# A linear-attention recurrence in levels: both head parities on the partitions, k masked in place of r

## The chip, the cores and the metric

The kernel runs on one core of a Trainium2 chip. A core has a matrix engine (TensorE, PE in the profile; its weight loads are listed as PEld), a vector engine (VectorE, DVE), an activation engine (ScalarE, ACT), a general engine (GpSimd, POOL) and a queue engine that issues DMAs (SyncE, SP). Each engine has its own instruction queue and runs it in order; semaphores make one engine wait for another. The metric is the time of one execution in microseconds, as the device measures it. All data are fp32.

## The reference

Two layers run over 32 sequences of 128 positions with 512 features. Layer 0 is a cross-attention with normalised inputs. Layer 1 is a block of the RWKV kind: layer norm and token shift, low-rank mixes, projections to r, k, v, a gate g and a decay w, a recurrence with a 16 x 16 state for each of 32 heads, a group norm, an output projection and a feed-forward part. What matters here is the recurrence:

```python
def step(s, rkvw):
    r_t, k_t, v_t, w_t = rkvw
    a = k_t[..., :, None] * v_t[..., None, :]
    out = jnp.einsum('bhi,bhij->bhj', r_t, u * a + s)
    s = a + w_t[..., :, None] * s
    return (s, out)
```

So the output at position t is r_t against the sum, over earlier positions i, of k_i v_i, decayed by the product of the w between i and t, plus the start state decayed, plus the same position's product weighted by u.

## The kernel before, in words

**Tiling.** The sequences go in 8 groups (`NG`) of `G` = 4. Activations lie transposed: 128 features on the partitions (8 heads of 16), and N = 4 x 128 positions of the four sequences along the free dimension. The 512 features make `NC` = 4 chunks, so the recurrence is called 8 x 4 = 32 times (`recurrence`, called from `layer1`). Positions are treated in halves of `C` = 64.

**Levels instead of steps.** The recurrence is not run step by step. At the level l, each block of 2l positions is cut in two; the products of the r of its right half with the k of its left half make a piece of a 64 x 64 matrix per head (`at`), and after each level r in the right half and k in the left half are multiplied by the decays of their half (`twice`, which also halves the table of decay products, `tot`). Before the change the position itself (`x0`, `d0`), neighbours at distance one (`x1`, `d1`) and the level 2 (`x2`, `d2`) are made by elementwise products on DVE, followed by a matmul with `sum_bc`, which adds the 16 features of a head; the levels 4, 8, 16 and 32 (`LEVELS`) are made by TensorE.

**A level on TensorE.** A matmul contracts over 32 partitions, `q * DM` to `(q + 1) * DM`, which hold two heads, an even and an odd one. To keep them apart r is copied twice by ACT with a mask on the partitions (`par`): the copy `r2` holds, side by side, r of the even head with zeros in the odd one's rows, and the reverse, 32 columns each, since only right halves are wanted. For each of 4 sequences, 2 halves `n` and 4 head pairs `q` one matmul has k as stationary operand (32 partitions x 64 positions) and r2 as moving operand (64 columns); the halves n go to the partitions 0 to 63 and 64 to 127 of four PSUM banks `pa[q]`. DVE then copies the wanted entries to `at` under a mask (`copy_predicated`); at the level 32 ACT copies them.

**After the levels.** v is transposed and copied into `vp` in a spaced form: 32 columns for each head pair and parity, half of them zero, with positions of both halves n on the partitions. The value products are `at` against `vp`, in two bunches of 32 matmuls: each contracts over the 64 positions of one half. The state for the second half (`s1`) needs k of the first half transposed (`kt`, 64 partitions), a product with v (`ps`) and a merge under the parity mask (two DVE operations). State products with r are added in the same banks `po`. The result is `acc`.

**What sets the order.** Every operation is first recorded (`Program.record`), with a cost for its engine (`cost`, or a number of ns given with `K.bunch`, which keeps a series of matmuls together), and `schedule` then lists the operations of all engines in an order of its own: it simulates the engines and the slots of the buffers, and moves work earlier where TensorE would idle. The instructions are emitted in that order by `Program.run`, line 229, so nearly every instruction of the profile has line 229; groups are told apart by the names of what they write and read. Buffers come from rings: 54 tiles of 128x512 (`t`), 8 PSUM banks (`bank`), two `rk` tiles with r and k, two `at` tiles for each q, two `vp` tiles, and 4 weight slots (`wring`).

The bunches around the change are: a level, `K.bunch(843)` at lines 887 to 898; the value products, `K.bunch(720)` twice at 983 to 995; the state products, `K.bunch(1020)` at 971; and the new state's product, `K.bunch(385)` at 952.

Of the kernel before, what the change touches and what calls it, by code (L numbers as in the profile page):

```python
# [13 lines left out]
AF = mybir.ActivationFunctionType  # L14
ALU = mybir.AluOpType
# [3 lines left out]
P = 128  # L19
B = 32  # L20
L = 128
E = 512
S = 16
G = 4
NG = B // G
N = G * L
# [2 lines left out]
NH = E // S  # L29
DM, NMIX, DD = 32, 5, 64  # L30
C = 64
LEVELS = (4, 8, 16, 32)
T_SLOTS, SMALL_SLOTS, W_SLOTS = 54, 40, 4
Q4 = 4
EPS = 1e-5

# [503 lines left out]
def xattn_then_rwkv(ctx: ExitStack, tc: tile.TileContext, a: dict, out: bass.AP):  # L540
# [5 lines left out]
    def slots(tag, count, shape, space=const):  # L546
        return [space.tile(shape, F32, tag=f"{tag}{i}", name=f"{tag}{i}") for i in range(count)]
# [4 lines left out]
    rks = Pool(slots("rk", 2, [P, 2 * N]))  # L552
# [18 lines left out]
    ident = const.tile([P, P], F32, tag="ident", name="ident")  # L571
# [29 lines left out]
    sum_bc, par = fixed("sum_bc", [P, H8, S]), fixed("par", [P, 2])  # L601
# [7 lines left out]
    def v_(name, c):  # L609
        i = VECS.index(name)  # L610
        return vec[:, i, c : c + 1]
# [218 lines left out]

    def recurrence(c, ex, xk, xr, xv, wk, wr, s0m):

        rk = View(Tensor(rks, [P, 2, N]))
        r, k = rk[:, 0], rk[:, 1]
        K.scalar.copy(r, proj(wr, xr, c))
        K.scalar.copy(k, proj(wk, xk, c))
        v = wt()
        K.scalar.copy(v, proj(wv, xv, c))

        vp = View(Tensor(vps, [P, G * Q4 * 2 * DM]))
        at = [View(Tensor(p, [P, G * 2, C])) for p in ats]
        pt = bank()
        for b in range(G):
            K.tensor.transpose(pt[:, b * P : (b + 1) * P], v[:, b * P : (b + 1) * P], ident)
        K.scalar.copy(
            vp.view(0, (2 * DM, G * Q4), (DM + S, 2), (1, S)),
            pt.rearrange("p (x y j) -> p x y j", x=G * Q4, y=2),  # L850
        )


        x0, x1 = wt(), wt()
        K.vector.scalar_tensor_tensor(x0, k, v_("u", c), r, ALU.mult, ALU.mult)
        K.vector.tensor_tensor(x1[:, 0 : N // 2], r[:, 1::2], k[:, 0::2], ALU.mult)
        sums = sum_bc.rearrange("p h s -> p (h s)")
        d0, d1 = bank(), bank()
        K.tensor.matmul(d0, sums, x0, start=True, stop=True)
# [1 line left out]
        acc = wt()  # L861

        def twice(h, tot):


            nb = N // (2 * h)
            s = rk.view(h, (N - h, 2), (2 * h, nb), (1, h))
            K.vector.tensor_tensor(s, s, tot.view(0, (1, 2), (2, nb), (0, h)), ALU.mult)
            got = wt([P, nb]) if nb > 64 else st_(nb)
            K.vector.tensor_tensor(got, tot[:, 0 : 2 * nb : 2], tot[:, 1 : 2 * nb : 2], ALU.mult)  # L870
            return got

        tot = twice(1, ex)

        nb = N // 4
        x2 = wt()
        K.vector.tensor_tensor(
            x2.view(0, (4, nb), (2, 2), (1, 2)),
            rk.view(2, (4, nb), (1, 2), (0, 2)),
            rk.view(N, (4, nb), (0, 2), (1, 2)), ALU.mult,  # L880
        )
        d2 = bank()
        K.tensor.matmul(d2, sums, x2, start=True, stop=True)
        tot = twice(2, tot)

        for li, l in enumerate(LEVELS):

            r2 = wt([P, G * 2, C])
            nb = C // (2 * l)
            for x in range(2):  # L890
                K.scalar.activation(
                    r2.view(x * (C // 2), (C, G * 2), (l, nb), (1, l)),
                    rk.view(l, (C, G * 2), (2 * l, nb), (1, l)),
                    AF.Identity, scale=par[:, x : x + 1],
                )
            pa = [bank() for _ in range(Q4)]
            with K.bunch(843):
                for b in range(G):
                    for n in range(2):
                        for q in range(Q4):  # L900
                            rows_q = slice(q * DM, (q + 1) * DM)
                            K.tensor.matmul(
                                pa[q][n * C : (n + 1) * C, b * C : (b + 1) * C],
                                rk[rows_q, 1, b * L + n * C : b * L + (n + 1) * C],
                                r2[rows_q, 2 * b + n],
                                start=True, stop=True,
                            )
            for q in range(Q4):
                if l < C // 2:
                    K.vector.copy_predicated(  # L910
                        at[q].view(l, (C, 2 * G), (2 * l, nb), (1, l)),
                        level[l].view(0, (0, 2 * G), (l, nb), (1, l)),
                        pa[q].view(0, (C // 2, 2 * G), (l, nb), (1, l)),
                    )
                else:
                    for n in range(2):
                        sl = slice(n * C, n * C + l)
                        K.scalar.copy(
                            at[q][sl, :, l : 2 * l],
                            pa[q][sl, 0 : N // 2].rearrange("p (x t) -> p x t", t=l),  # L920
                        )
            tot = twice(l, tot)
            if li == 0:
                t1, t2 = wt(), wt()
# [5 lines left out]
                nb = N // 4  # L930
                K.vector.tensor_tensor(
                    t2.view(0, (4, nb), (2, 2), (1, 2)),
                    d2.view(0, (4, nb), (2, 2), (1, 2)),
                    v.view(0, (4, nb), (0, 2), (1, 2)), ALU.mult,
                )
# [10 lines left out]
        pk = bank()  # L946
        for b in range(G):
            K.tensor.transpose(pk[0:C, b * P : (b + 1) * P], k[:, b * L : b * L + C], ident)
        kt = wt([C, N])
        K.scalar.copy(kt, pk[0:C, :])  # L950
        ps = bank()
        with K.bunch(385):
            for b in range(G):
                for q in range(Q4):
                    K.tensor.matmul(
                        ps[q * DM : (q + 1) * DM, b * DM : (b + 1) * DM],
                        kt[:, b * P + q * DM : b * P + (q + 1) * DM],
                        vp[0:C].view((b * Q4 + q) * 2 * DM, (DM + S, 2), (1, S)),
                        start=True, stop=True,
                    )  # L960
        s1 = wt([P, G, 2 * S])
        for x in range(2):
            of_x = (x * S, (2 * S, G), (1, S))
            K.vector.scalar_tensor_tensor(
                s1.view(*of_x), ps.view(*of_x), par[:, x : x + 1], s0t.view(*of_x),
                ALU.mult, ALU.add,
            )


        po = [bank() for _ in range(2)]  # L970
        with K.bunch(1020):
            for b in range(G):
                for n in range(2):
                    for q in range(Q4):
# [5 lines left out]
                            r[sl, b * L + n * C : b * L + (n + 1) * C],  # L980
                            start=(b == 0), stop=False, skip_group_check=True,
                        )
        for half in range(2):
            with K.bunch(720):
                for b in range(half * G // 2, (half + 1) * G // 2):
                    for x in range(2):
                        for n in range(2):
                            for q in range(Q4):
                                sl = slice(n * C, (n + 1) * C)
                                i = (b * Q4 + q) * 2 * DM + x * DM  # L990
                                K.tensor.matmul(
                                    po[n][q * DM : (q + 1) * DM, b * C : (b + 1) * C],
                                    vp[sl, i : i + DM], at[q][sl, 2 * b + x, :],
                                    start=False, stop=(x == 1), skip_group_check=True,
                                )
        for n in range(2):
            o = acc.view(n * C, (L, G), (1, C))
            K.vector.tensor_tensor(
# [263 lines left out]
```

## Time and profile before

| what | value |
|---|---|
| median of 3 runs | 1839.58 us (1839.23 to 1839.6) |
| the profiled execution | 1843.41 us |
| its span | 1841.7 us |
| PE busy | 1796.9 us (98%) |
| PE weight loads busy | 888.9 us (48%) |
| DVE busy | 1227.2 us (67%) |
| ACT busy | 751.2 us (41%) |
| POOL busy | 309.8 us (17%) |

The profile comes from one execution. The span runs from the first to the last instruction. Groups of instructions are listed with what they write and read (`bank<-t,rk` writes a PSUM bank and reads a t tile and an rk tile), for matmuls with the rows and columns of the array in use (`32*64`) and the moving operand (`32x64`), the count, the busy time in us, the mean ns of one instruction, and the idle time of the engine ahead of them with what ended it. Every fp32 matmul appears twice, each time with a weight load, and transposes once. The ends of matmuls are modelled, so a matmul's listed length includes the way through the array, and pieces are best measured from start to start. One group of four sequences takes about 228 us; its recurrence stage, from the first level to the last of its four calls, about 100 us (334 to 435 us in the second group).

### The profile page before, as it was taken

To read this page: it belongs to the slowest core of one execution; us is meant where nothing else is said; L and a number is where in the kernel's file an instruction comes from. 1 tells how busy PE (TensorE), PEld (TensorE's weight loads), DVE (VectorE), ACT (ScalarE), POOL (GpSimd) and SP (SyncE) were. 2 spreads that over 40 slices of the span, in tenths; PEclk is the share of its full clock that TensorE was granted. 3 is DMA by queue.
4 is the path that set the end of the run, shared out by engine and by line. 5 is a ranking of instruction groups with operands and counts; after the bars stand their busy time and mean duration, and the time that the engine had idled before them with its cause. 6 is when DMAs were issued, how large, how long until landed. Compare 5 with 4: busy or idle time off the path is not lost.

```text
span 1841.7 us, 46377 instructions
## 1 busy us (share of the span) xinstructions
PE 1796.9 (98%) x20264; PEld 888.9 (48%) x20264; DVE 1227.2 (67%) x2754; ACT 751.2 (41%) x1501; POOL 309.8 (17%) x329
## 2 busy tenths in 40 slices
PE   8999999999999999999999999999999999999998
PEld 4345543555435554355543555435554455445543
DVE  8857883678746786567855678556784567866652
ACT  5345621546225462254522644225452355425421
POOL 2420014000150001500025000240002400240011
PEclk9999999999999999999999999999999999999999
DMA  7001102021110201211011120111201111001000
GB/s 229 1 25 47 52 23 92 25 64 35 46 69 25 73 26 46 69 38 60 25 52 63 40 71 13 52 63 40 71 13 57 58 40 48 2 23 48 26 18 29
DMA packets 61947, 87.29 MB, mean 47 GB/s; under 512 B 20336, under 2 KB 21488, under 8 KB 61744
## 3 DMA queue, kind: packets, MB, share of 16 engines
q1 hardware_dynamic: 61024, 84.06, 14.1%
q8 instruction: 159, 2.61, 0.6%
q14 instruction: 44, 0.36, 0.1%
q10 hardware_dynamic: 720, 0.26, 0.1%
HBM read 75.93 MB, written 8.39 MB: 46 GB/s over the span
## 4 chain that ended last, share of the span: by engine, by line
PE 89%; DVE 6%; ACT 2%; POOL 2%; issue 1%; POOLq 0%; DVEq 0%; ACTq 0%
PE bank L229 89%; DVE t L229 5%; ACT t L229 1%; POOL t L229 1%; DVE small L229 1%; ACT at L229 0%; POOL small L229 0%; DVE at L557 0%; DVE rk L229 0%; DVE at L229 0%; POOLq L1258 0%; ACT L229 0%; DVE vp L557 0%; ACT rk L229 0%; DVE fold L229 0%
## 5 line engine op out<-in xcount | busy, mean ns | idle before, releaser
L229 PE MATMUL bank<-t,wring 128*128 128x512 f32 x1024 | 488.4, 605 | 4.0 <-ACT t L229 2.0
L229 PE MATMUL bank<-wring,t 128*128 128x512 f32 x768 | 341.0, 601 | 8.5 <-DVE t L229 8.5
L229 POOL TENSOR_TENSOR t<-t,t 128x512 f32<-128x512 f32 x192 | 242.8, 1299 | 435.1 <-DVE t L229 422.5
L229 DVE TENSOR_TENSOR t<-bank,t 128x512 f32<-128x512 f32 (+1 forms) x256 | 147.2, 585 | 225.6 <-PE bank L229 194.7
L229 PEld LDWEIGHTS bank<-t,wring 128*128 128x128 f32 x1024 | 182.0, 190 | 221.2 <-issue 167.7
L229 PE MATMUL bank<-t,t 128*128 128x512 f32 x512 | 261.6, 614 | 1.2 <-ACT t L229 1.2
L229 POOL TENSOR_TENSOR small<-small,neg_half 128x1 f32<-128x1 f32 (+1 forms) x96 | 59.3, 632 | 1091.6 <-DVE small L229 1072.7
L229 PEld LDWEIGHTS bank<-wring,t 128*128 128x128 f32 x768 | 146.3, 192 | 197.9 <-issue 179.5
L229 ACT ACTIVATE t<-bank 128x512 f32<-128x512 f32 x120 | 71.8, 598 | 368.2 <-PE bank L229 368.0
L229 ACT COPY t<-bank 128x512 f32<-128x512 f32 (+1 forms) x240 | 135.1, 587 | 201.7 <-PE bank L229 200.3
L229 ACT ACTIVATE t<-rk,par 128x256 f32<-128x256 f32 x256 | 116.7, 501 | 130.0 <-DVE rk L229 116.3
L229 PE MATMUL bank<-ident,t 128*128 128x128 f32 x900 | 140.5, 278 | 6.8 <-DVE t L229 6.7
L229 ACT ACTIVATE t<-bank,small 128x512 f32<-128x512 f32 x128 | 87.9, 689 | 140.4 <-DVE small L229 139.9
L229 PEld LDWEIGHTS bank<-ident,t 128*128 128x128 f32 x900 | 104.3, 140 | 81.1 <-issue 46.4
L229 DVE COPY_PREDICATED at<-level,bank 128x256 f32<-128x256 int32 x384 | 142.7, 426 | 0.0
L229 DVE SCALAR_TENSOR_TENSOR t<-bank,vec,t 128x512 f32<-128x512 f32 x192 | 131.3, 742 | 16.1 <-PE bank L229 16.1
L229 PEld LDWEIGHTS bank<-t,rk 32*64 32x64 f32 x8192 | 99.7, 130 | 82.3 <-ACT t L229 54.3
L229 PE MATMUL bank<-t,wv 128*128 128x512 f32 x256 | 128.6, 601 | 0.0
L229 PEld LDWEIGHTS bank<-t,t 128*128 128x128 f32 x512 | 85.0, 191 | 77.9 <-issue 35.9
L229 PE MATMUL bank<-t,rk 32*64 32x64 f32 x8192 | 117.9, 230 | 2.9 <-issue 2.9
L229 DVE TENSOR_REDUCE small<-bank 128x1 f32<-128x512 f32 x128 | 87.8, 686 | 41.1 <-PE bank L229 40.6
L229 ACT COPY at<-bank 32x256 f32<-32x256 f32 x256 | 87.8, 361 | 24.1 <-PE bank L229 21.3
(94 smaller groups left out, 1882.5 us busy)
## 6 DMA issues: line engine op xcount, KB each, us to landing
t<-in_ctx_dram SPq DMA_DIRECT2D x32, 256.0 KB, 3.1
t<-in_x_dram SPq DMA_DIRECT2D x32, 256.0 KB, 2.8
wring<-in_WrT_dram SPq DMA_DIRECT2D x8, 1024.0 KB, 5.3
wring<-in_WkT_dram SPq DMA_DIRECT2D x8, 1024.0 KB, 5.2
wring<-in_WgT_dram SPq DMA_DIRECT2D x8, 1024.0 KB, 5.0
wring<-in_WoT_dram SPq DMA_DIRECT2D x8, 1024.0 KB, 5.3
out_dram<-t SPq DMA_DIRECT2D x32, 256.0 KB, 2.0
wring<-in_WfkT_dram SPq DMA_DIRECT2D x7, 1024.0 KB, 5.0
```

The source lines that it names most:

```text
L229: f(*[real(x) for x in args], **{k: real(x) for k, x in kw.items()})
```

## The change

The two head parities move from the moving operand to the stationary one, and so to the partitions of the result.

- The `rk` tile grows from 2N to 3N columns: r, then k twice for each half of 64 positions, once with the odd heads' rows zeroed and once with the even heads'. Two masked ACT copies from the projection's PSUM bank write k; the masked copies of r at each level go.
- A level's matmul has 32 partitions x 128 columns of k as stationary operand and the 32 right-half positions of r, read in place, as moving operand. The result has 128 partitions (parity, position) x 32 columns.
- The level 2 becomes a TensorE level as well: `LEVELS` begins with 2, and the products `x2`, `d2`, `t2` go.
- `twice` multiplies k on DVE (two operations for the levels 2 to 16, one for 1 and 32), and r on GpSimd (POOL).
- `vp` is written by four copies of 64 partitions; parity and position are its partitions. The value products become one bunch of 32 matmuls over 128 partitions.
- k of the first half is transposed with both parities, and `s1` is one addition.
- The ring of t tiles has 52 tiles in place of 54.

```diff
-LEVELS = (4, 8, 16, 32)
-T_SLOTS, SMALL_SLOTS, W_SLOTS = 54, 40, 4
+LEVELS = (2, 4, 8, 16, 32)
+T_SLOTS, SMALL_SLOTS, W_SLOTS = 52, 40, 4
...
-        K.scalar.copy(k, proj(wk, xk, c))
+        pk = proj(wk, xk, c)
+        for x in range(2):
+            K.scalar.activation(
+                rk.view(N + x * C, (2 * C, 2 * G), (1, C)),
+                pk.rearrange("p (n s) -> p n s", s=C), AF.Identity, scale=par[:, x : x + 1],
+            )
...
-        K.scalar.copy(
-            vp.view(0, (2 * DM, G * Q4), (DM + S, 2), (1, S)),
-            pt.rearrange("p (x y j) -> p x y j", x=G * Q4, y=2),
-        )
+        for n in range(2):
+            for x in range(2):
+                K.scalar.copy(
+                    vp[x * C : (x + 1) * C].view(
+                        n * Q4 * DM + x * S, (2 * Q4 * DM, G), (DM, Q4), (1, S)
+                    ),
+                    pt[n * C : (n + 1) * C].view(x * S, (P, G), (DM, Q4), (1, S)),
+                )
...
-        K.vector.scalar_tensor_tensor(x0, k, v_("u", c), r, ALU.mult, ALU.mult)
-        K.vector.tensor_tensor(x1[:, 0 : N // 2], r[:, 1::2], k[:, 0::2], ALU.mult)
+        K.vector.scalar_tensor_tensor(x0, pk, v_("u", c), r, ALU.mult, ALU.mult)
+        K.vector.tensor_tensor(x1[:, 0 : N // 2], pk[:, 0::2], r[:, 1::2], ALU.mult)
...
-            nb = N // (2 * h)
-            s = rk.view(h, (N - h, 2), (2 * h, nb), (1, h))
-            K.vector.tensor_tensor(s, s, tot.view(0, (1, 2), (2, nb), (0, h)), ALU.mult)
+            nb, of = N // (2 * h), C // (2 * h)
+            if of == 1 or h == 1:
+                k2 = rk.view(N, (2 * C, 2 * G), (C, 2), (2 * h if h == 1 else 1, of if h == 1 else h))
+                by = tot.view(1, (2 * of, 2 * G), (0, 2), (2 if h == 1 else 0, of if h == 1 else h))
+                K.vector.tensor_tensor(k2, k2, by, ALU.mult)
+            else:
+                for x in range(2):
+                    k2 = rk.view(N + x * C, (2 * C, 2 * G), (2 * h, of), (1, h))
+                    by = tot.view(1, (2 * of, 2 * G), (2, of), (0, h))
+                    K.vector.tensor_tensor(k2, k2, by, ALU.mult)
+            r1 = rk.view(h, (2 * h, nb), (1, h))
+            K.gpsimd.tensor_tensor(r1, r1, tot.view(0, (2, nb), (0, h)), ALU.mult)
...
-        x2 = wt()
-        K.vector.tensor_tensor(
-            x2.view(0, (4, nb), (2, 2), (1, 2)),
-            rk.view(2, (4, nb), (1, 2), (0, 2)),
-            rk.view(N, (4, nb), (0, 2), (1, 2)), ALU.mult,
-        )
-        d2 = bank()
-        K.tensor.matmul(d2, sums, x2, start=True, stop=True)
...
-            r2 = wt([P, G * 2, C])
-            for x in range(2):
-                K.scalar.activation(
-                    r2.view(x * (C // 2), (C, G * 2), (l, nb), (1, l)),
-                    rk.view(l, (C, G * 2), (2 * l, nb), (1, l)),
-                    AF.Identity, scale=par[:, x : x + 1],
-                )
...
                             K.tensor.matmul(
-                                pa[q][n * C : (n + 1) * C, b * C : (b + 1) * C],
-                                rk[rows_q, 1, b * L + n * C : b * L + (n + 1) * C],
-                                r2[rows_q, 2 * b + n],
+                                pa[q][:, i : i + C // 2],
+                                rows[:, N + 2 * at_ : N + 2 * at_ + 2 * C],
+                                rows.view(at_ + l, (2 * l, nb), (1, l)),
                                 start=True, stop=True,
                             )
...
-                t2.view(0, (4, nb), (2, 2), (1, 2)),
-                d2.view(0, (4, nb), (2, 2), (1, 2)),
-                v.view(0, (4, nb), (0, 2), (1, 2)), ALU.mult,
-            right = acc.view(2, (4, nb), (1, 2))
-            for s in range(2):
-                K.vector.tensor_tensor(right, right, t2.view(s, (4, nb), (2, 2)), ALU.add)
...
-        for x in range(2):
-            of_x = (x * S, (2 * S, G), (1, S))
-            K.vector.scalar_tensor_tensor(
-                s1.view(*of_x), ps.view(*of_x), par[:, x : x + 1], s0t.view(*of_x),
-                ALU.mult, ALU.add,
-            )
+        K.vector.tensor_tensor(
+            s1, ps[:, 0 : G * DM].rearrange("p (b x) -> p b x", b=G), s0t, ALU.add
+        )
...
-        for half in range(2):
-            with K.bunch(720):
-                for b in range(half * G // 2, (half + 1) * G // 2):
-                    for x in range(2):
-                        for n in range(2):
-                            for q in range(Q4):
-                                sl = slice(n * C, (n + 1) * C)
-                                i = (b * Q4 + q) * 2 * DM + x * DM
-                                K.tensor.matmul(
-                                    po[n][q * DM : (q + 1) * DM, b * C : (b + 1) * C],
-                                    vp[sl, i : i + DM], at[q][sl, 2 * b + x, :],
-                                    start=False, stop=(x == 1), skip_group_check=True,
-                                )
+        with K.bunch(1000):
+            for b in range(G):
+                for n in range(2):
+                    for q in range(Q4):
+                        i = ((2 * b + n) * Q4 + q) * DM
+                        K.tensor.matmul(
+                            po[n][q * DM : (q + 1) * DM, b * C : (b + 1) * C],
+                            vp[:, i : i + DM], at[q][:, 2 * b + n, :],
+                            start=False, stop=True, skip_group_check=True,
+                        )
```

More of the change, by code (lines that the diff above doesn't have):

```diff
@@ L551, in xattn_then_rwkv @@
     small = Pool(slots("small", SMALL_SLOTS, [P, 64]))
-    rks = Pool(slots("rk", 2, [P, 2 * N]))
+    rks = Pool(slots("rk", 2, [P, 3 * N]))
     weights = Pool(slots("wring", W_SLOTS, [P, NC * E]))
@@ L831, in recurrence @@
     def recurrence(c, ex, xk, xr, xv, wk, wr, s0m):
-        rk = View(Tensor(rks, [P, 2, N]))
-        r, k = rk[:, 0], rk[:, 1]
+        rk = View(Tensor(rks, [P, 3 * N]))
+        r = rk[:, 0:N]
         K.scalar.copy(r, proj(wr, xr, c))
-        K.scalar.copy(k, proj(wk, xk, c))
+        pk = proj(wk, xk, c)
[4 more added lines that the diff above has]
+            )
         v = wt()
         K.scalar.copy(v, proj(wv, xv, c))
-        vp = View(Tensor(vps, [P, G * Q4 * 2 * DM]))
+        vp = View(Tensor(vps, [P, G * 2 * Q4 * DM]))
         at = [View(Tensor(p, [P, G * 2, C])) for p in ats]
@@ L873, in recurrence @@
         tot = twice(1, ex)
-        nb = N // 4
-        x2 = wt()
-        K.vector.tensor_tensor(
-            x2.view(0, (4, nb), (2, 2), (1, 2)),
-            rk.view(2, (4, nb), (1, 2), (0, 2)),
-            rk.view(N, (4, nb), (0, 2), (1, 2)), ALU.mult,
-        )
-        d2 = bank()
-        K.tensor.matmul(d2, sums, x2, start=True, stop=True)
-        tot = twice(2, tot)
         for li, l in enumerate(LEVELS):
-            r2 = wt([P, G * 2, C])
+            pa = [bank() for _ in range(Q4)]
             nb = C // (2 * l)
-            for x in range(2):
-                K.scalar.activation(
-                    r2.view(x * (C // 2), (C, G * 2), (l, nb), (1, l)),
-                    rk.view(l, (C, G * 2), (2 * l, nb), (1, l)),
-                    AF.Identity, scale=par[:, x : x + 1],
-                )
-            pa = [bank() for _ in range(Q4)]
             with K.bunch(843):
@@ L900, in recurrence @@
                         for q in range(Q4):
-                            rows_q = slice(q * DM, (q + 1) * DM)
+                            rows = rk[q * DM : (q + 1) * DM]
+                            at_ = b * L + n * C
+                            i = (2 * b + n) * (C // 2)
                             K.tensor.matmul(
-                                pa[q][n * C : (n + 1) * C, b * C : (b + 1) * C],
-                                rk[rows_q, 1, b * L + n * C : b * L + (n + 1) * C],
-                                r2[rows_q, 2 * b + n],
+                                pa[q][:, i : i + C // 2],
+                                rows[:, N + 2 * at_ : N + 2 * at_ + 2 * C],
+                                rows.view(at_ + l, (2 * l, nb), (1, l)),
                                 start=True, stop=True,
@@ L915, in recurrence @@
                 else:
-                    for n in range(2):
-                        sl = slice(n * C, n * C + l)
+                    for x in range(2):
+                        sl = slice(x * C, x * C + l)
                         K.scalar.copy(
@@ L923, in recurrence @@
             if li == 0:
-                t1, t2 = wt(), wt()
+                t1 = wt()
                 K.vector.tensor_tensor(acc, d0, v, ALU.mult)
@@ L929, in recurrence @@
                 K.vector.tensor_tensor(acc[:, 1::2], acc[:, 1::2], t1[:, 0 : N // 2], ALU.add)
-                nb = N // 4
-                K.vector.tensor_tensor(
-                    t2.view(0, (4, nb), (2, 2), (1, 2)),
-                    d2.view(0, (4, nb), (2, 2), (1, 2)),
-                    v.view(0, (4, nb), (0, 2), (1, 2)), ALU.mult,
-                )
-                right = acc.view(2, (4, nb), (1, 2))
-                for s in range(2):
-                    K.vector.tensor_tensor(right, right, t2.view(s, (4, nb), (2, 2)), ALU.add)
         s0t = wt([P, G, 2 * S])
@@ L945, in recurrence @@
         )
-        pk = bank()
+        pt = bank()
         for b in range(G):
-            K.tensor.transpose(pk[0:C, b * P : (b + 1) * P], k[:, b * L : b * L + C], ident)
-        kt = wt([C, N])
-        K.scalar.copy(kt, pk[0:C, :])
+            K.tensor.transpose(
+                pt[:, b * P : (b + 1) * P], rk[:, N + 2 * b * L : N + 2 * b * L + 2 * C], ident
+            )
+        kt = wt()
+        K.scalar.copy(kt, pt)
         ps = bank()
@@ L954, in recurrence @@
                 for q in range(Q4):
+                    i = (2 * b * Q4 + q) * DM
                     K.tensor.matmul(
                         ps[q * DM : (q + 1) * DM, b * DM : (b + 1) * DM],
-                        kt[:, b * P + q * DM : b * P + (q + 1) * DM],
-                        vp[0:C].view((b * Q4 + q) * 2 * DM, (DM + S, 2), (1, S)),
+                        kt[:, b * P + q * DM : b * P + (q + 1) * DM], vp[:, i : i + DM],
                         start=True, stop=True,
@@ L982, in recurrence @@
                         )
-        for half in range(2):
-            with K.bunch(720):
-                for b in range(half * G // 2, (half + 1) * G // 2):
-                    for x in range(2):
-                        for n in range(2):
-                            for q in range(Q4):
-                                sl = slice(n * C, (n + 1) * C)
-                                i = (b * Q4 + q) * 2 * DM + x * DM
-                                K.tensor.matmul(
-                                    po[n][q * DM : (q + 1) * DM, b * C : (b + 1) * C],
-                                    vp[sl, i : i + DM], at[q][sl, 2 * b + x, :],
-                                    start=False, stop=(x == 1), skip_group_check=True,
-                                )
+        with K.bunch(1000):
[7 more added lines that the diff above has]
+                            start=False, stop=True, skip_group_check=True,
+                        )
         for n in range(2):
```

## The prediction

> **What bounds the kernel now.** I read the page's first part and its chain of waits, then the groups with shapes kept apart, then the timeline of one recurrence. First the page: TensorE (PE) is busy for 98% of the span, and the chain that ended last is 89% PE.
>
> ```profile
> span 1841.7 us, 46377 instructions
> PE 1796.9 (98%) x20264; PEld 888.9 (48%) x20264; DVE 1227.2 (67%) x2754; ACT 751.2 (41%) x1501; POOL 309.8 (17%) x329
> PE 89%; DVE 6%; ACT 2%; POOL 2%; issue 1%; POOLq 0%; DVEq 0%; ACTq 0%
> ```
>
> So PE time added or removed moves the end one for one, and the other engines have room: DVE a third, ACT more than half, POOL four fifths. The chain in order of time says the same of the stage that is changed: one unbroken stretch of PE work covers the first levels.
>
> ```profile
> 306.89 73.81 PE bank L229 x814
> ```
>
> Next, what PE spends on the pieces that the change touches. These are timeline lines (start, length, ..., tile rows*columns, moving operand, count). A length includes the tail of the last matmul, so a piece costs the distance to the next start.
>
> ```profile
> 334.48 0.91 PE L229 MATMUL bank<-t,rk 32*64 32x64 f32 x64
> 335.32 1.12 PE L229 MATMUL bank<-t,wv 128*128 128x512 f32 x2
> ...
> 350.27 0.46 PE L229 MATMUL bank<-vp,t 64*32 64x32 f32 x32
> 350.65 1.12 PE L229 MATMUL bank<-t,t 128*128 128x512 f32 x2
> 351.71 1.09 PE L229 MATMUL bank<-rk,t 32*32 32x64 f32 x64
> 352.74 1.13 PE L229 MATMUL bank<-t,wring 128*128 128x512 f32 x2
> 353.79 0.86 PE L229 MATMUL bank<-at,vp 64*32 64x64 f32 x64
> 354.58 1.12 PE L229 MATMUL bank<-t,t 128*128 128x512 f32 x2
> ```
>
> A level (32 matmuls, 64 in the trace because each fp32 matmul appears twice, with two weight loads) takes 335.32 - 334.48 = 0.84 us; half of the value products 0.79; the state products 352.74 - 351.71 = 1.03; the new state's product 0.38. Last, the weight loads (PEld) by width, and the loads of the one group that already uses 32-row, 128-column tiles:
>
> ```profile
> L229 PEld LDWEIGHTS bank<-t,rk 32*64 32x64 f32 x8192 | 99.7, 130 | 82.3 <-ACT t L229 54.3 <-issue 22.5 <-ACT at L229 2.0
> L229 PEld LDWEIGHTS bank<-rk,t 32*32 32x32 f32 x2048 | 30.0, 105 | 19.9 <-issue 11.5 <-DVE t L229 6.0 <-DVE at L229 1.5
> L229 PEld LDWEIGHTS bank<-t,w2a 32*128 32x128 f32 x256 | 10.1, 183 | 21.7 <-DVE t L229 7.6 <-issue 7.1 <-DVE small L229 5.3
> 308.80 0.31 PEld L229 LDWEIGHTS bank<-t,w2a 32*128 32x128 f32 x8 [0.76 <-DVE t L229]
> 910.63 1.05 PE L229 MATMUL bank<-wol,t 128*128 128x128 f32 x8
> ```
>
> A load of 32 columns lasts 105 ns, of 64 130, of 128 183: about 0.81 ns a column. Eight loads of 128 columns, two on each of four row tiles, take 0.31 us. The four tiles load side by side (one after another would take far longer), but the second load of a tile begins only when the first has passed: 0.31 - 0.18 leaves 0.13, less some 0.02 for the fourth tile's later start, so about **0.11 us per load and tile**. That fits 128 x 0.81 = 0.104.
>
> **The change part by part (PE).**
>
> *Level products.* A level stays 32 matmuls, but each loads 32x128 weights and streams 32 columns, where it loaded 32x64 and streamed 64. The eight tiles of 32*64 become four of 32*128, so a tile takes 16 loads in place of 8. Streaming is cheap: 512-column matmuls on full tiles go at 0.43 us each in the trace (the 32 from 914.96 on take 14.00 us), so 0.84 ns a column, and 32 columns are 0.027 us against a load of 0.108. I price the level by its loads: 16 x 0.108 = 1.73, plus what a bunch has around its steady part. The state bunch gives that: 16 rounds of 64 columns on four tiles are 16 x 0.0535 = 0.86 of its 1.03, so 0.17. Together 1.90 us. From below, with start and tail hidden, 1.73. From above, load and matmul one after the other in a tile: 16 x (0.108 + 0.027) + 0.17 = 2.33. I take 1.90, because the load is covered by the matmul elsewhere in the trace: the eight 128-column instructions above on one full tile take 1.05 us, (1.05 - 0.29) / 7 = 0.109 each (0.29 is the mean of one), with a load of 0.108 and a stream of 0.107 each. There are five levels in place of four, and 8 x 4 = 32 recurrences: 5 x 1.90 x 32 = 304.0 against 4 x 0.84 x 32 = 107.5: **+196.5 us**.
>
> The Trainium skill ("TensorE: Matmul & The Clock Gate", The mechanism, in the part on row and column tiling) says that a weight load overlaps running matmuls only where their row group differs. In a level the load that follows on a tile always has the row group of that tile's matmul, so by this rule load and matmul would add and the total would be about 2060, the upper price. The 0.109 us row, load and matmul on the same rows, disagrees, and I go by the row.
>
> *The pair level's product.* The d2 matmul (128x512, two instructions of 0.43) goes: 0.86 x 32 = **-27.3 us**.
>
> *Value products.* Two bunches of 0.79 become one of 32 matmuls, each 128*32 with 64 columns on four column tiles. The state bunch has this count, width of load and stream: 1.03. Bounds: 0.86 (streams alone) and 1.2 (the state bunch with another 0.17). -(1.58 - 1.03) x 32 = **-17.6 us**.
>
> *Others.* The new state's product keeps 16 matmuls on four column tiles; the k transpose doubles its width of load but not its stream (four cost 0.63 with 64-column weights, 0.66 with 128): 0. Bunches per recurrence stay eight (5 + 1 + 1 + 1 against 4 + 1 + 1 + 2), so the changes of tile shape around them cost the same.
>
> Sum on PE: 196.5 - 27.3 - 17.6 = **+151.6 us**.
>
> **The other engines**, which cost nothing while PE covers them:
>
> - ACT: 256 masked copies of r go (116.7 us busy); k takes two masked 128x512 activations for one copy (+0.7 us), vp four 64x256 copies of about 0.36 for one of 0.59 (+0.9): -116.7 + 51 = -65 us.
> - DVE: four more predicated copies per recurrence (142.7 us over 384, so 0.37 each: +1.5 us); the pair level's product, its value product and two adds go (0.68 + 0.68 + 2 x 0.42 = 2.2); the doublings of k alone take two operations of 0.69 and eight of 0.42, 4.7 against 6 x 0.69 = 4.1; s1 is one operation for two (-0.25). About -0.35 us each: -11 us.
> - POOL: 192 doublings of r, 128x256, at half of the 1.30 us row: +125 us, to about 435 of 1990.
>
> *A wait that is added.* Each doubling of r now runs on POOL while DVE doubles k, and the next level waits for both. The two engines disturb each other: a DVE operation that reads only SBUF takes 0.42 us alone, and here took 1.50 behind POOL, which was busy from 321.72 for 2.96 us.
>
> ```profile
> 323.47 1.50 DVE L229 TENSOR_TENSOR t<-rk 128x256 f32<-128x256 f32 x1
> 321.72 2.96 POOL L229 TENSOR_TENSOR t<-t,t 128x512 f32<-128x512 f32 x2
> ```
>
> From the end of one level's matmuls to the next level's start the chain is then at worst 0.65 (POOL) + 2 x 0.42 (DVE) + about 0.3 of lags = 1.8 us. Before, it was DVE 0.69, then ACT's masked copies of 0.50 each, with three lags: 2.1. In the changed kernel's PE order, priced by the rows above, the work between two levels of one recurrence is 2.1 us or more nearly everywhere, so it covers 1.8. Queued behind a late k on DVE are the predicated copies, which only the value products need. From below the change of chain gains nothing, since PE had no gap there; a few of the 45 us that PE now idles may go (at most 10). From above, with no cover, 6 x 0.65 x 32 = 125 us. I take 0: the row of cover is above the chain. The k bank is read by two ACT and two DVE operations, about 2.6 us, before it is free, in place of 0.6; four banks of a level are held as before and d2's is gone, so I put 0 on it as well.
>
> The profiled execution took 1843.4 us (span 1841.7 and 1.7 around it); the median of the three runs, 1839.58, is 0.2% below. 1843.4 + 151.6 = 1995, or from the median **1991 us**, 8.2% slower.
>
> **The rivals.**
>
> *Faster: the level is bound by the number of its instructions, not by load width.* The 64 loads and 64 matmuls might go at the 0.84 us of now, as the 32-column bunches nearly do. Then 5 x 0.84 x 32 = 134.4, and 134.4 - 107.5 - 27.3 - 17.6 = -18: 1822 us. It decides below a level price of (107.5 + 27.3 + 17.6) / 160 = 0.95 us. Against it stands the 0.11 us between two loads of one tile; for it, that no row has 128-column loads with a stream as short as 32.
>
> *Loads and matmuls add:* 2.33 x 160 - 152.4 = +220: 2060 us. Against it the 0.109 row; for it again the short stream, behind which nothing in the trace stands.
>
> *POOL and DVE in each other's way:* the chain outgrows its cover. Half of the 125 us on top gives 2053, all of it 2116. For it the 1.50 us row, and cover of only 2.1 to 2.6 us in about half of the gaps; against it, ACT's step leaving the chain.
>
> **How the numbers follow.** The forecast has 0.73, loads adding 0.10, the POOL chain 0.08, the instruction-bound level 0.08; 0.01 is left for a sum that happens to cancel. The forecast's own range is 1957 (level at 1.75, so 280 - 152.4 = +127.6, and 10 us of idle gone) to 2040 (level at 1.96, +161, and a third of the POOL price). Taking in loads that add, the range is 1957 to 2065; it leaves out the faster case, the cancelling sum and most of the POOL one. Within 0.2% of 1839.6 this kernel can't be told from no change. Faster 0.08, same 0.01, slower 0.91.
>
> **What would show it.** In the changed profile: the group bank<-rk 32*128 with 32 moving columns, 10240 in the trace, near 1.9 us from start to next start, its loads at 183 ns and about 0.11 us apart on a tile; PEld's busy time up by more than 150 us; the value products near 1.03; sum_bc 128x512 halved; ACT down by about 65 us, POOL near 435; PE's idle time still about 45 us. I am wrong if a level takes less than 0.95 us, or if PE idles over 80 us with POOL or DVE named as the releaser.

## The result, and the profile after

The changed kernel takes **2015.39 us** (median of 4 runs, 2013.4 to 2016.39) against 1839.4 us for the kernel before: a ratio of 1.0957, with a 95% interval of 1.0938 to 1.0976. The forecast was 1991 us with a range of 1957 to 2065: the direction, and six sevenths of the size (+152 of +176 us).

The page of the changed kernel, in its first part and its chain:

```profile
span 2013.5 us, 46658 instructions
PE 1966.2 (98%) x20200; PEld 1081.7 (54%) x20200; DVE 1247.1 (62%) x2851; ACT 690.5 (34%) x1373; POOL 493.9 (25%) x527
PE 85%; DVE 6%; POOL 3%; ACT 2%; DMA 2%; issue 1%; SPq 0%; POOLq 0%; DVEq 0%; ACTq 0%
```

PE is busy for 98% as before, so the kernel is still bound by PE and has 169 us more of it. PEld's busy time rose by 193 us. The timeline of PE shows where (start, length, ..., count):

```profile
370.04 1.99 PE L229 MATMUL bank<-rk 32*128 32x32 f32 x64
371.96 2.84 PE L229 MATMUL bank<-t,wring 128*128 128x512 f32 x6
...
382.78 1.10 PE L229 MATMUL bank<-at,vp 128*32 128x64 f32 x64
383.81 1.98 PE L229 MATMUL bank<-t,t 128*128 128x512 f32 x4
```

A level takes 371.96 - 370.04 = 1.92 us, where it took 0.84; the value products take 1.03 in one bunch, where they took 1.58 in two. The timeline of the weight loads, for the first quarter of that level:

```profile
370.04 0.54 PEld L229 LDWEIGHTS bank<-rk 32*128 32x128 f32 x16 [0.76 <-issue]
```

Sixteen loads are four on each of four tiles (a tile is here the part of the array, 32 rows by 128 columns, that one matmul uses): 0.54 less the 0.19 of the last and the 0.02 by which the fourth tile starts later leaves 0.33 for three steps, 0.11 us from load to load.

The other engines, by groups (busy us, mean ns of one):

```profile
L229 PEld LDWEIGHTS bank<-rk 32*128 32x128 f32 x10240 | 311.2, 192 | 108.4 <-issue 87.4 <-POOL rk L229 11.4 <-ACT vp L229 4.5
L229 DVE COPY_PREDICATED at<-level,bank 128x256 f32<-128x256 int32 x512 | 229.9, 503 | 0.0
L229 POOL TENSOR_TENSOR rk<-rk,t 128x256 f32<-128x256 f32 x96 | 96.2, 1002 | 403.8 <-PE bank L229 300.9 <-DVE t L229 66.1 <-ACT t L229 12.9
L229 POOL TENSOR_TENSOR rk<-rk,small 128x256 f32<-128x256 f32 x96 | 85.9, 895 | 366.1 <-PE bank L229 338.5 <-issue 27.6
```

The predicated copies and POOL's doublings of r are dearer than forecast. The idle time ahead of the loads names POOL's `rk` for 11.4 us, but no wait of PE itself does (total us, times, longest):

```profile
PE bank L229 <- DVE t L229: 18.4, 33, 1.1
PE bank L229 <- ACT t L229: 12.6, 22, 1.8
PE bank L588 <- DMA WoT<-in_WoT_dram: 6.0, 1, 6.0
PE bank L229 <- DVE rk L229: 1.4, 1, 1.4
PE bank L229 <- POOL t L229: 1.2, 6, 0.2
PE bank L229 <- ACT at L229: 0.7, 1, 0.7
PE bank L229 <- DVE bol L593: 0.6, 1, 0.6
PE bank L229 <- issue: 0.6, 3, 0.2
```

What is new lies near the end. The view of one stretch (length, busy time of PE, PEld, DVE, ACT and POOL, granted clock, DMA) shows PE at half clock for 30.7 us.

```profile
1868.80:1899.50 30.70, 27.71 (x549) 26.23 (x548) 18.13 (x46) 4.12 (x11) 5.48 (x7) 0.50 0.01 2
```

The timeline of PE has levels one after the other there:

```profile
1868.51 7.54 PE L229 MATMUL bank<-rk 32*128 32x32 f32 x128
1877.46 10.88 PE L229 MATMUL bank<-rk 32*128 32x32 f32 x196 [1.40 <-DVE rk L229]
```

Two levels that follow each other take 7.54 us there, 3.8 each. PE is listed as busy for 27.7 of the 30.7 us, and none of its gaps is longer than 1.4 us. The stretch did not begin with a wait either: in the 3.41 us before it (1865.37 to 1868.78), at full clock, PE was listed as busy for 3.39.

For all runs I split the span of the profiled execution in three. Idle is the span less PE's busy time. The time at half clock comes from the trace's clock records (the mean clocks of 0.995 before and 0.989 after say the same). **Work** is the span less the idle time and less half of the time at half clock, so PE's work as it would take at full clock. It is approximate: where PE waits at half clock, a part is taken off twice.

| kernel | median us | span | idle | at half clock (longest) | work |
|---|---|---|---|---|---|
| before | 1839.4 | 1841.7 | 44.8 | 19.8 (3.4) | 1787.0 |
| after | 2015.4 | 2013.5 | 47.3 | 47.7 (30.7) | 1942.3 |
| wide stream (64 columns) | 2016.5 | 2014.7 | 46.7 | 41.8 (20.5) | 1947.1 |
| full stream (128 columns) | 2009.1 | 2007.5 | 46.9 | 20.8 (3.8) | 1950.2 |
| half load | 1882.0 | 1881.0 | 52.5 | 55.8 (10.2) | 1800.5 |
| measured costs in the plan | 1973.6 | 1970.5 | 27.3 | 11.9 (5.1) | 1937.3 |
| 1400 ns in the plan | 2005.7 | 2004.5 | 40.6 | 35.2 (23.9) | 1946.4 |
| level 2 on DVE | 1993.1 | 1990.7 | 51.1 | 56.0 (6.8) | 1911.6 |
| level 2 on DVE, measured costs | 1986.2 | 1982.5 | 44.2 | 78.4 (10.2) | 1899.1 |
| r doubled on DVE | 2001.6 | 2005.6 | 38.7 | 44.1 (10.2) | 1944.8 |
| before, measured costs | 1875.8 | 1875.0 | 63.5 | 27.0 (6.8) | 1798.0 |

From before to after the work grows by 155.3 us, the idle time by 2.5, and the clock takes 14.0 more (half of 27.9).

### The profile page after: what moved, and what is told of

Same layout as the page of the kernel before. It is cut to its first block, busy times and chain, and to the rows that moved or that the text cites. A ratio compares the mean times of both kernels' runs of the same rounds, so it can differ in the third digit from the quotient of the medians.

```text
span 2013.5 us, 46658 instructions
## 1 busy us (share of the span) xinstructions
PE 1966.2 (98%) x20200; PEld 1081.7 (54%) x20200; DVE 1247.1 (62%) x2851; ACT 690.5 (34%) x1373; POOL 493.9 (25%) x527
## 4 chain that ended last, share of the span: by engine, by line
PE 85%; DVE 6%; POOL 3%; ACT 2%; DMA 2%; issue 1%; SPq 0%; POOLq 0%; DVEq 0%; ACTq 0%
PE bank L229 85%; DVE t L229 5%; POOL t L229 3%; ACT t L229 2%; DMA t<-in_x_dram 2%; DVE small L229 1%; ACT L229 0%; DVE rk L229 0%; DVE at L557 0%; ACT at L229 0%; SPq L229 0%; POOL small L229 0%; ACT rk L229 0%; POOLq L1248 0%; DVE vp L557 0%
## 5 line engine op out<-in xcount | busy, mean ns | idle before, releaser
L229 PEld LDWEIGHTS bank<-rk 32*128 32x128 f32 x10240 | 311.2, 192 | 108.4 <-issue 87.4
L229 DVE TENSOR_TENSOR t<-bank,t 128x512 f32<-128x512 f32 (+2 forms) x256 | 133.8, 535 | 319.3 <-PE bank L229 285.3
L229 PE MATMUL bank<-rk 32*128 32x32 f32 x10240 | 328.9, 277 | 2.2 <-DVE rk L229 1.4
L229 ACT COPY t<-bank 128x512 f32<-128x512 f32 x240 | 132.8, 591 | 328.6 <-PE bank L229 324.4
L229 DVE COPY_PREDICATED at<-level,bank 128x256 f32<-128x256 int32 x512 | 229.9, 503 | 0.0
L229 POOL TENSOR_TENSOR rk<-rk,t 128x256 f32<-128x256 f32 x96 | 96.2, 1002 | 403.8 <-PE bank L229 300.9
L229 POOL TENSOR_TENSOR rk<-rk,small 128x256 f32<-128x256 f32 x96 | 85.9, 895 | 366.1 <-PE bank L229 338.5
L229 DVE TENSOR_TENSOR rk<-rk,small 128x256 f32<-128x256 f32 (+1 forms) x160 | 82.3, 514 | 144.0 <-PE bank L229 144.0
L229 DVE SCALAR_TENSOR_TENSOR t<-bank,vec,t 128x512 f32<-128x512 f32 x192 | 131.3, 742 | 23.9 <-PE bank L229 23.9
L229 DVE TENSOR_TENSOR rk<-rk,t 128x256 f32<-128x256 f32 (+1 forms) x160 | 81.1, 507 | 103.6 <-PE bank L229 99.5
```

The lines of the kernel that those rows point to most:

```text
L229: f(*[real(x) for x in args], **{k: real(x) for k, x in kw.items()})
```

## The experiments

**Is a level bound by its weight loads? A longer stream.** The stream goes from 32 columns to 64; the copies then read the same entries from their new places (not shown).

```diff
-                                pa[q][:, i : i + C // 2],
+                                pa[q][:, i : i + C],
                                 rows[:, N + 2 * at_ : N + 2 * at_ + 2 * C],
-                                rows.view(at_ + l, (2 * l, nb), (1, l)),
+                                rows[:, at_ : at_ + C],
...
```

> The changed kernel, with the level matmul streaming all 64 positions of r instead of the 32 of the right halves; the loads stay 32x128, the copies read the same entries as before. Theory (a level is bound by its 128-column loads, 16 a tile at 0.11 us): the longer stream hides behind the load, a level goes from 1.92 to 1.94 us at most, +4 us in all. If the 31 us at half clock near the end of the changed kernel come from how little the array streams, they go too and the time is about 2004 us; if not, 2019. Rival (load and stream add, or the strided read of r or the writing of PSUM sets the pace): 16 x 0.027 x 160 = +69 us, 2084 us, or a level twice as long where the writing sets it.

Measured: 2016.52 us, ratio 1.0968 (1.0952 to 1.0984), not to be told from the changed kernel. A level takes 372.70 - 370.76 = 1.94 us from start to start, some 0.03 more:

```profile
370.76 2.01 PE L229 MATMUL bank<-rk 32*128 32x64 f32 x64
372.70 0.70 PE L229 MATMUL bank<-t,wring 128*128 128x512 f32 x1
```

Twice the streaming costs next to nothing (5 us of work in the table): load and stream do not add, and neither the strided read of r nor the writing of PSUM sets the pace. The long stretch at half clock shrank from 30.7 to 20.5 us and did not vanish, which neither of my two numbers foresaw.

**A narrower load.** The stationary operand is cut to 64 columns. The products of the other parity, and their copies (not shown), are left out.

```diff
-                                pa[q][:, i : i + C // 2],
-                                rows[:, N + 2 * at_ : N + 2 * at_ + 2 * C],
+                                pa[q][0:C, i : i + C // 2],
+                                rows[:, N + 2 * at_ : N + 2 * at_ + C],
...
```

> The changed kernel, with the level's stationary operand cut to the 64 columns of one parity; the level products of the other parity, and their copies, are left out. Same count of matmuls, same streams of 32. Theory (bound by the width of the loads): a round of four tiles takes 0.058 us in place of 0.112, so a level takes 16 x 0.058 + 0.17 = 1.10 us, 160 x (1.92 - 1.10) = -131 us: 1884 us, and about 1869 if the stretch at half clock goes as well. Rival (bound by the count of instructions, or by the strided streams): a level stays at 1.92 us and the time at 2015 us.

Measured: 1881.99 us, ratio 1.0231 (1.0213 to 1.0249). The timeline of this run shows a level of 339.62 - 338.55 = 1.07 us, against 1.10 expected:

```profile
338.55 1.13 PE L229 MATMUL bank<-rk 32*64 32x32 f32 x64
339.62 1.98 PE L229 MATMUL bank<-t,wring 128*128 128x512 f32 x4
```

The count of matmuls and the streams are those of the changed kernel, so the **width of the weight load** is what a level pays for: 0.85 us a level, and 142 us of work in the table. The instruction-bound rival falls. The order of PE's groups came out different in this run, so the 133 us of its time are not the price of the levels alone; the 0.85 us of a level is.

**The stretch at half clock.** The stream is made as long as the load, 128 columns; the last matmul of every eight has 64.

```diff
-                                pa[q][:, i : i + C // 2],
+                                pa[q][:, i : min(i + 2 * C, N)],
                                 rows[:, N + 2 * at_ : N + 2 * at_ + 2 * C],
-                                rows.view(at_ + l, (2 * l, nb), (1, l)),
+                                rows[:, at_ : min(at_ + 2 * C, N)],
...
```

> The changed kernel, in its own order, with the level matmul streaming 128 columns (r of 128 positions, the upper 64 overwritten by the next matmul), so that the array streams nearly without a break while the loads are as before. Theory A (the long stretch at half clock comes from levels that follow each other and stream only a quarter of the time; 31 us long in the changed kernel, 20 us with streams of 64): the stretch falls to 7 us or none, worth 12 to 15 us, against 160 x 0.08 us = +13 us for levels of 2.0 us: 2012 to 2018 us, and no stretch. Theory B (the stretch comes from PE's waits in the last group, not from streaming): it stays at 20 us or more, and the time is 2023 us or more.

Measured: 2009.12 us, ratio 1.0917 (1.0900 to 1.0935): some 6 us *less* than the changed kernel, with nearly four times the streaming, and 3 us below theory A's band, where a level grew by 0.03 us and not by the 0.08 expected. The same stretch of its span:

```profile
1868.80:1899.50 30.70, 27.48 (x704) 22.71 (x702) 27.39 (x68) 8.02 (x18) 7.00 (x9) 1.00 0.01 3
```

And PE's timeline, a level in the open and the same levels one after the other:

```profile
370.55 2.01 PE L229 MATMUL bank<-rk 32*128 32x128 f32 x64
372.49 2.84 PE L229 MATMUL bank<-t,wring 128*128 128x512 f32 x6
...
1873.77 4.29 PE L229 MATMUL bank<-rk 32*128 32x128 f32 x128
1879.46 6.69 PE L229 MATMUL bank<-rk 32*128 32x128 f32 x196 [1.40 <-DVE rk L229]
```

The granted clock is 1.00, and two levels take 4.29 us in place of 7.54. PE's order is the same, its idle time is the same (46.9 us), and the 1.40 us wait for DVE's `rk` is still there. So these waits alone do not lower the clock; with them in place, the longer stream did away with the stretch, and thin streaming of levels that follow each other is what it needed. The mean clock says it in every execution: 0.995 in all four here, 0.988 to 0.990 in the four of the changed kernel. With 64 columns a wait may have had its part: there the stretch began at 1879.33, as the 1.40 us wait ended. A level at 1.94 us (372.49 - 370.55) is also the best test of load against stream: a load of 0.108 and a stream of 0.107 on the same tile go side by side.

**The order.** The planner is told what the bunches take.

```diff
-            with K.bunch(843):
+            with K.bunch(1917):
...
-        with K.bunch(1000):
+        with K.bunch(1030):
```

> The changed kernel, the planner told the measured times of the two bunches (1917 ns for a level, 1030 for the value products, in place of 843 and 1000), so that only the order changes. Theory (the time is PE work, and the order covers the waits): PE's idle time of 42 us moves by less than 10 us; with the levels of the last group placed otherwise the 31 us at half clock may go, worth 15 us: 2000 to 2015 us. Rival (the order, planned with a level at 0.84 us, loses time): 1975 us or less.

Measured: 1973.64 us, ratio 1.0734 (1.0717 to 1.0751). My theory fell here, and its rival's number held: 42 us come from the order alone. The table says how: 20 us of idle time go, and 36 us at half clock (18 us). (The expectation's 42 us of idle time is the sum of the waits listed above; the table's 47.3 counts every gap.) PE in this run's page:

```profile
span 1970.5 us, 46710 instructions
PE 1943.2 (99%) x20200; PEld 1069.6 (54%) x20200; DVE 1253.4 (64%) x2851; ACT 694.4 (35%) x1374; POOL 481.9 (24%) x527
```

Was it because the plan was nearer to the truth? Two runs ask that: one with the level's cost half-way, and the kernel before with its own measured costs.

```diff
-            with K.bunch(843):
+            with K.bunch(1400):
```

> The changed kernel, the planner told 1400 ns for a level, half-way between the 843 of the change and the 1917 that it takes. Theory A (the 42 us that the measured costs gained come from how far the plan is from the truth): about half of the gain, 1985 to 2000 us. Theory B (any other order would do: the changed kernel's is an unlucky one): anywhere from 1970 to 2015, no nearer to half than to either end.

Measured: 2005.67 us, ratio 1.0902 (1.0882 to 1.0921): a quarter of the gain, outside the band for half of it and within theory B's. Its order puts six levels one after the other, with no wait of PE before or among them, and from 1868.89 on the clock is halved for 23.9 us:

```profile
1863.20 18.14 PE L229 MATMUL bank<-rk 32*128 32x32 f32 x384
```

That is the stretch again, in another order.

The kernel before, with measured costs (two more costs are changed likewise, 1000 to 1071 and 1000 to 1103):

```diff
-            with K.bunch(720):
+            with K.bunch(788):
...
-        with K.bunch(1000):
+        with K.bunch(1071):
...
```

> The kernel before, the planner told the measured times of the bunches that differ from its plan (788 ns in place of 720 for half of the value products, 1071 and 1103 in place of 1000 for three others). Theory (its plan is near the truth, so there is little to gain): within 10 us of 1839 us. Rival (any plan gains from measured costs as the changed kernel's did): 1825 us or less, which would beat both kernels.

Measured: 1875.75 us, ratio 1.0193 (1.0175 to 1.0210): 36 us *slower* with truer costs, with 19 us more idle time and 11 us more work. Both of my numbers missed. So truer costs do not make a better order as a rule: changes of 7 to 10% in four planning costs gave an order that cost 36 us. Why one order idles less than another stays open; I tried no other way to vary it.

**Level 2 undone.** DVE makes level 2 again, first with the plan's costs of the change, then with measured ones.

```diff
-LEVELS = (2, 4, 8, 16, 32)
+LEVELS = (4, 8, 16, 32)
...
+        K.vector.tensor_tensor(
+            ku.rearrange("p (n s) -> p n s", s=C),
+            rk.view(N, (2 * C, 2 * G), (1, C)), rk.view(N + C, (2 * C, 2 * G), (1, C)), ALU.add,
+        )
...
+        K.tensor.matmul(d2, sums, x2, start=True, stop=True)
+        tot = twice(2, tot)
...
```

> The changed kernel with one part undone: level 2 is made by products on DVE and a matmul with sum_bc again (one more DVE addition rebuilds the unmasked k). Theory: 32 levels of 1.92 us go and 32 matmuls of 0.86 us come back, -61 + 27 = -34 us: 1981 us, DVE's work hidden. Rival (the level's cost is not its PE time but the chain through DVE and POOL between levels): the six doublings stay, so the time stays within 10 us of 2015, or rises by the DVE work, 32 x 2.9 = 93 us at most.

> Level 2 on DVE again, as in the earlier run, now with the measured costs of the bunches. Against the changed kernel with measured costs (1973.6 us). Theory (a level costs its PE time of 1.92, the order no longer in the way): -61 + 27 = -34 us: 1940 us. Rival (levels cost less than their PE time, as the earlier -22 suggests): -22 us, 1952 us.

Measured: 1993.07 us, ratio 1.0839 (1.0822 to 1.0855), so -22 us where -34 was expected and the rival had -10 at most; and 1986.17 us, ratio 1.0798 (1.0775 to 1.0822), 13 us *more* than the changed kernel with measured costs, which misses both numbers. Read by time alone the second contradicts the first. By the table the work falls by 31 and by 38 us, about the 34 expected, and the rest is order: the second run idles 17 us longer and spends 78 us at half clock, 66 more. Here too half clock follows levels in a row: PE was listed as busy throughout 445.20 to 448.61, and the next 10.24 us went at half clock.

```profile
445.13 7.88 PE L229 MATMUL bank<-rk 32*128 32x32 f32 x186 [0.27 <-DVE t L229]
```

The PE price of a level holds, and the net of a part can't be read from one order.

**POOL.** The doublings of r go to DVE.

```diff
-            K.gpsimd.tensor_tensor(r1, r1, tot.view(0, (2, nb), (0, h)), ALU.mult)
+            K.vector.tensor_tensor(r1, r1, tot.view(0, (2, nb), (0, h)), ALU.mult)
```

> The changed kernel, with the doublings of r on DVE in place of POOL (192 operations of 128x256, +80 us of DVE work, POOL back to about 310 us). Theory (POOL is hidden, it is not part of the time): PE's work at full clock (span less idle time less half of the time at half clock) stays within 6 us of the changed kernel's 1942, and PE's waits do not fall by more than 10 us. Rival (POOL and DVE in each other's way hold the next level up): PE's idle time of 47 us falls by 15 us or more, and the time with it, below 2000 us.

Measured: 2001.62 us, ratio 1.0876 (1.0858 to 1.0894). Work rose by 2.5 us and idle time fell by 8.6, within the theory's bounds and short of the rival's; the time came within 2 us of the rival's 2000. (The table has the longest of the four executions, 2007.4 us; they went from 1999.5 us on, with mean clocks of 0.990 to 0.994.) The order changed with the edit, and by the runs above that alone can move more. So POOL is not what makes the kernel slower than the one before; whether it costs some 10 us is open.

## Why the prediction was right, and where it was off

*What bounds the kernel.* PE, as said: PE's idle time is 47 us after 45, and the level and the value bunch were measured. With them the sum is 154.8 in place of 151.6, and the table's work grew by 155.3.

*The level products.* Forecast 1.90 us, measured 1.92: loads 0.11 us apart, streams hidden. Taken at 1.92 the term is +199.7 in place of +196.5. The two runs with longer streams and the one with the narrower load show it from both sides. The row that carried it was the low-rank group with its eight loads in 0.31 us, far away in the kernel, with the same 32x128 weights.

*The rule on row groups.* The forecast weighed a sentence of the Trainium skill ("TensorE: Matmul & The Clock Gate", The mechanism) against one row. The run with 128-column streams settles it for the loads and streams of this kernel, in which the next load on a tile overlaps the stream on the same rows: 1.94 us a level, where loads and streams one after the other would take 16 x (0.108 + 0.107) + 0.17 = 3.6.

*The pair level's product and the value products.* The 32 matmuls went, and the value bunch takes 1.03 us, as taken from the state bunch. What the 32 matmuls had cost was not measured apart from the rest. (0.86 x 32 is 27.5 and not 27.3, and the terms of the range's 2040 add up to 2042; neither slip has weight.)

*The clock, the term that was missing.* "Sum on PE" was made at full clock throughout, and gave no reason for it. The changed kernel lost 14 us more to half clock than the one before, nearly all in one stretch where the last recurrences have no other PE work between their levels. That is the larger part of the 24 us by which the forecast was short; 4 us are the sum's own, 2 the idle time, and 4 come from the start: the profiled execution before was 4 us above its median, the one after was not. The measured time lies inside the forecast's own range (to 2040) even so, but that range made room for a dearer level and for POOL, not for the clock, so there it held in part by luck. The Trainium skill ("TensorE: Matmul & The Clock Gate", HAM oscillation) gives as the rule that the clock falls after PE gaps of more than about 3.4 us. In this stretch no gap was above 1.4 us, so the measurement does not fit that rule; what the array streamed, not how long PE was listed as busy, decided. Waits well below that length precede half clock elsewhere: the nine stretches of 3.41 us inside the spans of the kernels before and after each followed 3.41 us in which PE was listed as busy for 1.3 to 2.7 us, with no wait above 2.3 us.

*The order.* The forecast took the cover between two levels from the changed kernel's order and put 0 on the rest. The idle time bears that out for this order, but a better one was to be had: 42 us of the 176 go with another order of the same work. Whether the kernel before has a better order too is open; the one other order that was run made it 36 us slower.

*ACT, DVE and POOL.* ACT fell by 61 us (forecast 65). DVE rose by 20 where -11 was forecast, above all because the predicated copies of the new level 2 are listed at 0.7 to 0.8 us each. By busy time the 128 new copies add 87 us, 0.68 each and not the 0.37 of the row that I used, some 40 us more than forecast; the rest of DVE's work came out some 9 us lower. POOL rose by 184 us and not by 125, at 0.95 us for a doubling of r in place of 0.65. Both are terms that were mis-sized. PE covers them, but for 10 us or so that the run with r doubled on DVE leaves open.

## What to carry to other kernels

Before a matmul is turned round so that its stationary operand gets wider and its stream shorter, price both sides per tile: here a load cost 0.11 us per 128 columns and was paid sixteen times a tile, while streams of 32, 64 and 128 columns made a difference of 0.03 us a level. Look for the price in any group with the same width of weights, however far off. Compare versions of a kernel with a planned order by work, idle time and clock, not by time alone: new costs in the plan made the changed kernel 42 us faster and the kernel before 36 us slower.

## What the runs showed of the hardware that was not expected

- The granted clock halved for 30.7 us while PE was listed as busy for 27.7 of them, in levels that loaded weights most of the time and streamed 32 columns a load. With 64 columns it was 20.5 us, with 128 no stretch above 3.8 us, at the same idle time, and the kernel with nearly four times the streaming was 6 us faster.
- Every stretch at half clock in the eleven traces, but for the last of each, which the end of the span cuts, lasted a whole multiple of 3.41 us: 3.41, 6.83, 10.24, 20.48, 23.89 and 30.72.
- A predicated copy of 128x256 into runs of two elements (level 2) takes 0.7 to 0.8 us; into runs of 4, 8 and 16 elements 0.42. In the run that made level 2 on DVE none was above 0.46.
- A 128x256 multiplication in place on POOL with a broadcast operand took 0.90 to 1.00 us, where 128x512 without one took 1.29. Whether the broadcast, the strided runs or DVE's work beside it makes the difference was not tried.
